# Layer 0's router logits as extra columns of the value and output projections, in a two-layer MetaFormer kernel

## The chip, the cores and the metric

The kernel runs on one core of a Trainium2 chip. A core has five engines that work beside each other, each on its own queue in order: TensorE (PE; its weight loads are shown as PEld), VectorE (DVE), ScalarE (ACT), GpSimd (POOL) and SyncE (SP), which here only issues DMAs. PE writes its results to PSUM, which has eight banks; VectorE and ScalarE evict them from there. The metric is the device time of one execution in microseconds (us), the median over runs. All data is float32 unless said otherwise.

## The reference

The input x has the shape (2, 256, 56, 56): two images, 256 channels, 3136 positions each, so 6272 tokens. Layer 0 computes

```
x = x + attention(ln_c(x))          # 8 heads of 32, window 7 x 7, projections wq wk wv wo with biases
t = tokens(x)                        # (2, 3136, 256)
u = ln_t(t)
logits = u @ router_w.T              # 8 experts
p = softmax(logits); the two largest, normed by their sum
t = t + u + sum over the two experts of p * (gelu(u @ w1 + b1) @ w2 + b2)
```

with `ln(v) = (v - mean) / sqrt(var + eps)` over the 256 channels (eps 1e-6 in ln_c, 1e-5 in ln_t). Layer 1 has two ternary 3 x 3 convolutions with batch norm in the place of attention, and again 8 experts (hidden size 512), of which each token takes two. Only layer 0 is touched by the change.

Two identities matter for it. A layer norm ahead of a linear map can be put behind it: with a matrix whose columns have mean zero, the mean drops out, and the norm is a factor per token. And attention's output enters the logits through wo alone, so `router_w` times `wo` can be multiplied once, ahead.

## The kernel before, in words

The image is cut into 14 strips (`STRIPS`, 7 per image) of 8 rows, that is 448 tokens, held as 4 blocks (`NTT`) of 112 (`TT`) tokens on the partitions.

*Attention (`score_*` and `att_*` pools).* The loop over strips g runs 8 chunks each (4 blocks of 14 columns times 2 halves of the heads). A chunk is `scores` (matmuls sc, two exponentials ex on ScalarE) and `attend` of the chunk before (matmuls av, added into `acc` by VectorE). Beside the chunks two kinds of generators are advanced, one step per chunk, up to their next `yield`: `project(g + 2)`, which norms a coming strip, turns it (px), and computes keys, queries (both pj) and values (pv); and everything in `under_way`, advanced by `push`. There `leave(g - 1)` finishes a strip behind: it loads its x again (`again`: xr plus the bias of wo, on POOL), writes the softmax denominators to DRAM (sums), loads them in another layout (den), inverts them (rden), sends them back out (shares) and loads them spread (rec), multiplies `acc` by them (oc, 8 VectorE operations), resets the strip's rows of `acc` for the second image (`fresh`), multiplies by wo (pw) and adds xr. Then `norm` of `routing(0)` norms the tokens (statistics on VectorE, the root as a power on POOL, scaling to u on ScalarE), turns u by 8 transposes (pu, evicted by two ScalarE copies), stores x + u as x_mid, and computes the logits with 8 matmuls (pl) of 8 columns, whose result VectorE copies to `lgs`. `settle`, for two strips at a time, finds the two best experts of each token on VectorE, counts places with small matmuls (rk), and scatters each token's row into the experts' list xs: 16 indirect DMAs on POOL, two a step (strips 12 and 13 are settled alone, 8 each).

The PSUM tiles with tag aux (px, pj, pv, pw, pu, pl, rk) take turns on two banks. pv and pw fill a bank with two blocks of 256 columns; VectorE evicts the two blocks of pv in two operations, those of pw in one of 512 columns.

*Experts of layer 0.* The rows of strips 0 to 9 (`FIRST`) are enough to know 27 tiles (`EARLY`) of 256 rows that one expert will surely have. They are planned (`plan_first`, `tiles0(0)`) as soon as these strips are counted, and the expert stage starts with them while strips 10 to 13 still go through `leave`, `norm` and `settle`: `beside(j)` advances `under_way` by one step per tile. When nothing is under way any more, `routed_all` plans the remaining 28 tiles (counts, and one small matmul pf behind the whole plan), frees attention's memory, and the preparation of the convolution weights (`ternary`) begins beside the tiles, with loads of the raw weights on SP and sums on ScalarE (low). Per tile, SP loads rows (xg, four tiles ahead) and weights (w, three tiles ahead), PE turns the rows (pt), multiplies twice (ph, py), VectorE adds the bias (y), and POOL scatters y to ys with two indirect DMAs. The order inside this stage is written out by hand; in the attention stage each engine's order is set by a scheduler from the program's order, which is the order of the steps above.

After that come the convolutions (from 835 us) and layer 1's experts, which the change doesn't touch.

Of the kernel before, what the change touches and what calls it, by code (L numbers as in the profile page):

```python
# [10 lines left out]
F32 = mybir.dt.float32  # L11
# [4 lines left out]
ALU = mybir.AluOpType  # L16
# [4 lines left out]
P = 128  # L21
# [608 lines left out]
def metaformer(ctx: ExitStack, tc: tile.TileContext, a: dict, out: bass.AP, flag):  # L630
# [98 lines left out]
    def routing(layer, wp, tp, ps):  # L729

        pre = f"L{layer}_ffn_"
        gate = wp.tile([P, KC, E], F32, tag="gate", name="gate")
        nc.sync.dma_start(gate, a[pre + "gate"].rearrange("(k p) e -> p k e", p=P))
        if layer == 1:
            gate_b = wp.tile([TT, E], F32, tag="gate_b", name="gate_b")
            nc.sync.dma_start(gate_b, a[pre + "gate_b"].partition_broadcast(TT))
# [11 lines left out]
        def norm(i, src, late=False):  # L748


            eng = nc.vector if late else small_eng
# [5 lines left out]
            scaled(u, src, rstd, nmr)  # L757
            yield
# [10 lines left out]
            if layer == 0:  # L769
                eng.tensor_tensor(src, src, u, ALU.add)  # L770
                nc.sync.dma_start(x_mid[i], src)
                yield
            lg = lgs[:, i * NTT : (i + 1) * NTT, :]
            pl = ps.tile([TT, NTT, E], F32, tag="pl" if layer else "aux", name="pl")
# [9 lines left out]
            if layer == 1:  # L784
                yield
                nc.vector.tensor_tensor(lg, pl, bcast(gate_b, 1, [TT, NTT, E]), ALU.add)
            else:
                nc.vector.tensor_copy(lg, pl)
# [209 lines left out]
        return norm, settle, tiles, gates, wgt, counted, sent  # L998
# [294 lines left out]
    with ExitStack() as st:  # L1293
# [22 lines left out]
        def again(g, eng):  # L1316

            xr[g] = tp.tile([TT, NTT, C], F32, tag="xr", name="xr")
            nc.sync.dma_start(xr[g], a["x_tok"][g])
            eng.tensor_tensor(xr[g], xr[g], bcast(bias["o"], 1, [TT, NTT, C]), ALU.add)  # L1320

# [3 lines left out]
        for n in "kqvo":  # L1325
            wt[n] = (aw if n == "o" else sw).tile([P, KC, C], F32, tag=f"w{n}", name=f"w{n}")
            nc.sync.dma_start(wt[n], a[f"L0_conv_w{n}"].rearrange("(k p) o -> p k o", p=P))
# [15 lines left out]
        nc.vector.tensor_copy(far_w.rearrange("p h w -> p (h w)"), far_f)  # L1343
        fits = aw.tile([TT, DEN], F32, tag="fits", name="fits")
# [18 lines left out]
        norm0, settle0, tiles0, gates0, wgt0, counted0, _ = routing(0, aw, tp, ps)  # L1363

        def project(g):
# [39 lines left out]
            for t in range(0, NTT, 2):  # L1405
                pj = ps.tile([TT, 2, C], F32, tag="aux", name="pv")
                for i in range(2):
                    for k in range(KC):
                        nc.tensor.matmul(  # L1409
                            pj[:, i, :],  # L1410
                            xc[:, k, (t + i) * TT : (t + i + 1) * TT],
                            wt["v"][:, k, :],
                            start=k == 0,
                            stop=k == KC - 1,
                        )
                for i in range(2):
                    nc.vector.tensor_tensor(
                        vals[g % 3][:, t + i, :, 0::3, :],
                        pj[:, i, :].rearrange("p (j i d) -> p j i d", i=2, d=HD),
                        bias["v"].rearrange("p (j i d) -> p j i d", i=2, d=HD),  # L1420
                        ALU.add,
                    )
                yield
# [54 lines left out]
        def leave(g):  # L1478
# [11 lines left out]
            rden = tp.tile([TT, DEN], F32, tag="rden", name="rden")  # L1490
            for i in range(2):
# [7 lines left out]
            nc.vector.reciprocal(rden, den)  # L1499
            nc.sync.dma_start(shares.rearrange("i (p n) -> (i p) n", n=DEN), rden)  # L1500
# [6 lines left out]

            fit = tp.tile([TT, DEN], F32, tag="fit", name="fit")
            nc.vector.tensor_scalar(fit, den, LEAST, None, ALU.is_ge)
            nc.vector.scalar_tensor_tensor(fit, den, MOST, fit, ALU.is_le, ALU.mult)  # L1510
            nc.vector.tensor_tensor(fits, fits, fit, ALU.add)
# [3 lines left out]
            for i in range(2):  # L1515
                at = slice(3 * HD * i, 3 * HD * i + HD)
                for j in range(2):
                    to = HD * (2 * j + i)
                    for k in range(KC):
# [5 lines left out]
                        )  # L1525
            if g < NS:
                fresh(s)
            yield
            for t in range(0, NTT, 2):
                pw = ps.tile([TT, 2, C], F32, tag="aux", name="pw")  # L1530
                for i in range(2):
                    for k in range(KC):
                        nc.tensor.matmul(  # L1533
                            pw[:, i, :],
                            oc[:, k, (t + i) * TT : (t + i + 1) * TT],
                            wt["o"][:, k, :],
                            start=k == 0,
                            stop=k == KC - 1,
                        )
                x = xr[g][:, t : t + 2, :]  # L1540
                nc.vector.tensor_tensor(x, pw, x, ALU.add)
# [28 lines left out]

        fresh(0)
# [3 lines left out]
        finish(project(1))  # L1575
        before = None
# [24 lines left out]
        while not plans0:  # L1601
            push()
            plan_first()
# [78 lines left out]
    with mid:  # L1682
# [133 lines left out]
        with ExitStack() as both:  # L1816
# [45 lines left out]
            norm, settle, tiles, gates, wgt1, _, sent = routing(1, wp, tp, ps)  # L1862
# [197 lines left out]
```

## Time and profile before

| what | value |
|---|---|
| runs, median of 6 | 1781.97 us (1775.02 to 1783.38) |
| profiled execution, its own time | 1774.22 us |
| its span, first to last instruction | 1772.4 us |
| mean granted TensorE clock | 0.899 |
| busy PE, PEld, DVE, ACT, POOL | 1529.9, 1208.7, 933.1, 712.4, 672.6 us |
| first px (strip 0) | 17.37 us |
| px of strip 13 | 419.80 us |
| first pt, layer 0's experts | 512.18 us |
| first and last issue of a late row's scatter | 576.45 and 652.49 us |
| first convolution matmul | 835.0 us |

The busy times are of one profiled execution and are averages over stages with different limits, so the stage has to be looked at before a share says anything. In the lists below, a line gives the engine, the line of the kernel, the operation and its tiles as out<-in; "us, times, longest" in a list of waits is the total, the number and the longest; matmuls of float32 appear as two records each (pv, pw, pl, pj), transposes as one.

### The profile page before, as it was taken

What the parts mean: (1) busy time and instruction counts of PE and PEld (TensorE: products, weight loads), DVE (VectorE), ACT (ScalarE), POOL (GpSimd) and SP (SyncE); (2) the same over time, 40 slices, a digit from 0 to 9 for tenths busy, and PEclk for the clock granted to TensorE, in tenths of its full rate; (3) what the DMA queues carried; (4) which work ended last, traced back from release to release, by engine and by line L of the source; (5) the groups of instructions that cost most, each with busy time, mean ns of one, the idle gap of its engine ahead of it and who ended that gap; (6) DMA issues with size and microseconds to landing.
All of it is one profiled execution on the core that took longest, in us unless ns stands there. A gap on an engine that the chain in (4) does not pass through costs nothing.

```text
span 1772.4 us, 26006 instructions
## 1 busy us (share of the span) xinstructions
PE 1529.9 (86%) x8709; PEld 1208.7 (68%) x8709; DVE 933.1 (53%) x2621; ACT 712.4 (40%) x1388; POOL 672.6 (38%) x676
## 2 busy tenths in 40 slices
PE   5999997999988958893899899967669999999964
PEld 3555664555567847782678788857558888888843
DVE  3457665566645437875788555568761111111136
ACT  2444442443433424643655452235434333333312
POOL 2111634335343763451455134316765222222210
PEclk9999997999879988996999999975669999999975
DMA  7122424122157967886552000024557877788758
GB/s 231 46 66 86 126 92 131 56 62 75 57 189 237 304 216 249 310 273 176 166 157 73 0 1 1 1 65 129 172 193 259 281 269 270 268 275 284 265 165 307
DMA packets 91886, 291.77 MB, mean 165 GB/s; under 512 B 20487, under 2 KB 35803, under 8 KB 80416
## 3 DMA queue, kind: packets, MB, share of 16 engines
q1 hardware_dynamic: 66736, 231.79, 41.1%
q0 software_dynamic: 21200, 51.82, 8.2%
q10 hardware_dynamic: 3808, 6.42, 1.0%
q8 instruction: 70, 1.15, 0.3%
q14 instruction: 72, 0.59, 0.1%
HBM read 218.51 MB, written 74.20 MB: 165 GB/s over the span
## 4 chain that ended last, share of the span: by engine, by line
PE 62%; DVE 14%; DMA 10%; issue 7%; POOL 4%; ACT 2%; SPq 1%; POOLq 0%; DVEq 0%; ACTq 0%
PE ph L1091 14%; PE py L1108 13%; PE pc L1753 12%; PE av L1464 4%; PE sc L1435 3%; PE pj L1387 3%; PE pw L1533 3%; DVE oc L1520 3%; PE pv L1409 3%; PE pt L1059 2%; DMA got<-ys 2%; DMA out<-o_out 2%; PE pl L777 2%; POOL ys L1118 1%; DVE t_stats L700 1%
## 5 line engine op out<-in xcount | busy, mean ns | idle before, releaser
L1091 PE MATMUL ph<-ut,w 128*128 128x256 f32 (+1 forms) x1472 | 309.4, 361 | 1.8 <-DMA w<-in_L_experts 1.8
L1108 PE MATMUL py<-w,h 128*128 128x256 f32 x1288 | 298.1, 380 | 0.0
L1116 DVE TENSOR_TENSOR y<-py,w 128x512 f32<-128x512 f32 (+1 forms) x120 | 76.8, 640 | 405.5 <-PE py L1108 405.1
L1091 PEld LDWEIGHTS ph<-ut,w 128*128 128x128 f32 x1472 | 252.0, 195 | 28.8 <-DMA w<-in_L_experts 2.4
L1753 PE MATMUL pc<-hi,wq 128*128 128x448 f32 x672 | 256.0, 382 | 16.9 <-ACT hi L1724 16.9
L860 POOL DMA_INDIRECT xs<-u,pos x224 | 217.4, 970 | 131.4 <-issue 60.7
L1108 PEld LDWEIGHTS py<-w,h 128*128 128x128 f32 x1288 | 243.8, 191 | 32.5
L1753 PE MATMUL pc<-lo,wq 128*128 128x448 f32 x672 | 254.9, 380 | 0.0
L1118 POOL DMA_INDIRECT ys<-y,dest x136 | 135.9, 999 | 232.9 <-DVE dest L1066 173.8
L1098 ACT ACTIVATE h<-ph,w 128x256 f32<-128x256 f32 (+1 forms) x368 | 162.9, 448 | 102.1 <-PE ph L1091 98.0
L1454 ACT ACTIVATE ex<-sc 112x476 f32<-112x476 f32 (+3 forms) x224 | 116.3, 571 | 203.9 <-PE sc L1444 197.5
L1063 ACT COPY ut<-pt 128x512 f32<-128x512 f32 (+1 forms) x120 | 65.2, 544 | 281.1 <-PE pt L1059 279.3
L1723 POOL TENSOR_TENSOR v<-pad 128x928 f32<-128x928 f32 (+1 forms) x56 | 98.3, 1761 | 159.6 <-DVE lo L1725 146.9
L1753 PEld LDWEIGHTS pc<-hi,wq 128*128 128x128 f32 x672 | 129.1, 192 | 32.2 <-ACT hi L1724 18.2
L1753 PEld LDWEIGHTS pc<-lo,wq 128*128 128x128 f32 x672 | 129.3, 192 | 15.4 <-DVE lo L1725 1.0
L1464 PE MATMUL av<-ex,vals 112*64 112x238 f32 (+3 forms) x896 | 124.0, 399 | 12.7 <-DVE acc L1474 12.5
L1118 POOL DMA_INDIRECT ys<-y,to x81 | 84.4, 1041 | 128.0 <-DVE dest L1066 65.8
L1474 DVE TENSOR_TENSOR acc<-av,acc 128x238 f32<-128x238 f32 (+3 forms) x224 | 87.8, 408 | 68.2 <-PE av L1464 66.3
L1464 PEld LDWEIGHTS av<-ex,vals 112*64 112x64 f32 x896 | 56.6, 142 | 61.9 <-issue 25.9
L1724 ACT CAST hi<-v 128x928 fp32r<-128x928 f32 x56 | 54.1, 966 | 110.4 <-PE pc L1753 104.2
L1435 PE MATMUL sc<-q_im,keys 32*112 32x238 f32 (+3 forms) x896 | 91.5, 428 | 2.2 <-ACT ex L1454 2.0
L713 POOL TENSOR_TENSOR t_rstd<-t_mv,eps 112x4 f32<-112x4 f32 x26 | 5.6, 217 | 208.8 <-DVE t_mv L702 208.8
(237 smaller groups left out, 2267.5 us busy)
## 6 DMA issues: line engine op xcount, KB each, us to landing
w<-in_L_experts SPq DMA_DIRECT2D x64, 1154.0 KB
w<-in_L_experts SPq DMA_DIRECT2D x56, 641.0 KB
xg<-xs SPq DMA_DIRECT2D x97, 260.0 KB
got<-ys SPq DMA_DIRECT2D x28, 896.0 KB
acc<-in_fresh SPq DMA_DIRECT2D x14, 896.0 KB
xt<-in_x_tok SPq DMA_DIRECT2D x14, 448.0 KB
xr<-in_x_tok SPq DMA_DIRECT2D x14, 448.0 KB
rec<-shares SPq DMA_DIRECT2D x28, 224.0 KB
```

The costliest lines, as they stand in the source:

```text
L860: w = nc.gpsimd.indirect_dma_start(xs[:, :], bass.IndirectOffsetOnAxis(ap=pos[:, j, t0 + t : t0 + t + 1], axis=0), us[t // NTT][:, t % NTT ...
L1091: nc.tensor.matmul(ph[:, :g], w1[:, k, f * P : (f + 1) * P], d["ut"][:, k, :g], start=k == 0, stop=k == KC - 1,)
L1098: nc.scalar.activation(d["h"][:, f, :g], ph[:, :g], AF.Gelu, bias=b1[:, f : f + 1])
L1108: nc.tensor.matmul(py[:, i, :], d["h"][:, f, i * P : (i + 1) * P], w2[:, f, :], start=f == 0, stop=f == NF - 1,)
L1116: nc.vector.tensor_tensor(y[:, :gp], py[:, :gp], bcast(b2, 1, [P, gp, C]), ALU.add)
L1118: o = nc.gpsimd.indirect_dma_start(ys[:, :], bass.IndirectOffsetOnAxis(ap=d["to"][:, i : i + 1], axis=0), y[:, i, :], None, bounds_check=T ...
L1435: nc.tensor.matmul(sc[h // 2][:, h % 2, :nq], keys[g][p, c, tx * TT : (tx + 1) * TT], q_im[p, c, r0:r1, c0:c1], start=True, stop=False,)
L1454: nc.scalar.activation(e[:, :, :nq], sc[j][:, :, :nq], AF.Exp, scale=HD**-0.5)
L1464: nc.tensor.matmul(av[VW * i : VW * (i + 1), :nq], vals[g % 3][:, tx, 2 * c + j, 2 * i : 2 * i + 2, :].rearrange("p a d -> p (a d)"), ex[j ...
L1474: nc.vector.tensor_tensor(d, av[:, :nq].rearrange("p (h w) -> p h w", w=c1 - c0), d, ALU.add)
L1723: (nc.gpsimd if u else nc.vector).tensor_tensor(v[:, :, at : at + n, :], *r, op)
L1753: nc.tensor.matmul(pc[:, :NT], wq[:, k, c, dx * C + o * P : dx * C + (o + 1) * P], part[:, k, :, dx : dx + W], start=m == 0, stop=m == 2 * ...
```

## The change

1. `norm` of layer 0 no longer turns u and multiplies it by the gate: pu, its two copies, pl and its copy are gone. `lgs` of a strip is instead multiplied by rstd (on POOL, on VectorE for strips 12 and 13), and x_mid is stored in a step of its own.
2. wv and wo get 8 columns more (256 + 8). Those of wv are the gate with its column means taken off (`gates_of_values`), those of wo are wo times these (`gates_of_output`); both are made once, at the start, with 8 small matmuls (pg, po, pb) and a load of wo's rows. pv and pw are then 264 columns wide and fill one bank per block, four banks a strip each instead of two.
3. Each bank has two evictions, both on VectorE: the 256 columns as before, and the 8 columns into `lgs` (for pv times the strip's standard deviation `dev`, for pw added). `again` adds the part of the bias `lg_b` to `lgs`, on POOL.
4. In `leave`, for strips 0 to 9 (`calm`), xr's load has a step to itself, ahead of the step that issues sums and den, and the step that inverts den ends there; shares and rec are issued in the next. `fresh` moves behind the yield that follows oc.
5. The expert stage is begun when strip 9's rows are all scattered in the program's order, not when the first plan exists.

```diff
@@ norm
+            lg = lgs[:, i * NTT : (i + 1) * NTT, :]
+            if layer == 0:
+                eng.tensor_tensor(lg, lg, bcast(rstd, 2, [TT, NTT, E]), ALU.mult)
+                yield
+                eng.tensor_tensor(src, src, u, ALU.add)
+                yield
+                nc.sync.dma_start(x_mid[i], src)
+                return
             yield
             ut = tp.tile([P, KC, NT], F32, tag="ut", name="ut", bufs=1)
...
-            if layer == 0:
-                eng.tensor_tensor(src, src, u, ALU.add)
-                nc.sync.dma_start(x_mid[i], src)
-                yield
...
@@ again
+            lg = lgs0[:, g * NTT : (g + 1) * NTT, :]
+            eng.tensor_tensor(lg, lg, lg_b, ALU.add)
@@ at the start
+        wo_rows = parts[:, 2:].rearrange("p a j n -> p (a j n)")[:, : KC * C]
+        free = wt["v"][:, :, C:]
+        def gates_of_values():
+            pg = ps.tile([P, E], F32, tag="aux", name="pg")
+            for k in range(KC):
+                nc.tensor.matmul(pg, ones, gate[:, k, :], start=k == 0, stop=k == KC - 1)
+            nc.vector.tensor_scalar_mul(mean, pg, -1.0 / C)
+            nc.vector.tensor_tensor(free, gate, bcast(mean, 1, [P, KC, E]), ALU.add)
+        def gates_of_output():
+            nc.sync.dma_start(wo_rows, a["L0_conv_wo_rows"].rearrange("(k p) c -> p k c", p=P))
+            nc.sync.dma_start(bo, a["L0_conv_bo"])
+            po = ps.tile([P, KC, E], F32, tag="aux", name="po")
+            for k in range(KC):
+                for o in range(KC):
+                    nc.tensor.matmul(po[:, k, :], wo_rows[:, o, k * P : (k + 1) * P], free[:, o, :], ...)
+            nc.vector.tensor_copy(wt["o"][:, :, C:], po)
+            for k in range(KC):
+                nc.vector.tensor_scalar_mul(gate[:, k, :], free[:, k, :], bo[:, k : k + 1])
+            pb = ps.tile([TT, E], F32, tag="aux", name="pb")
+            for k in range(KC):
+                nc.tensor.matmul(pb, ones[:, :TT], gate[:, k, :], start=k == 0, stop=k == KC - 1)
+            nc.vector.tensor_copy(lg_b, bcast(pb, 1, [TT, NTT, E]))
@@ project
-            for t in range(0, NTT, 2):
-                pj = ps.tile([TT, 2, C], F32, tag="aux", name="pv")
...
+            nc.vector.reciprocal(dev, rstd)
+            for t in range(NTT):
+                pj = ps.tile([TT, C + E], F32, tag="aux", name="pv")
...
+                nc.vector.tensor_scalar_mul(lgs0[:, g * NTT + t, :], pj[:, C:], dev[:, t : t + 1])
+                if t % 2:
+                    yield
@@ leave
+            calm = g < FIRST[0]
+            if calm:
+                yield
             for i in range(2):
                 nc.sync.dma_start(sums[i : i + 1, :]...
...
             nc.vector.reciprocal(rden, den)
+            fit = tp.tile([TT, DEN], F32, tag="fit", name="fit")
...
+            if calm:
+                yield
             nc.sync.dma_start(shares.rearrange("i (p n) -> (i p) n", n=DEN), rden)
...
+            yield
             if g < NS:
                 fresh(s)
-            yield
-            for t in range(0, NTT, 2):
-                pw = ps.tile([TT, 2, C], F32, tag="aux", name="pw")
...
-                nc.vector.tensor_tensor(x, pw, x, ALU.add)
+            for t in range(NTT):
+                pw = ps.tile([TT, C + E], F32, tag="aux", name="pw")
...
+                nc.vector.tensor_tensor(x, pw[:, :C], x, ALU.add)
+                lg = lgs0[:, g * NTT + t, :]
+                nc.vector.tensor_tensor(lg, pw[:, C:], lg, ALU.add)
@@ after the loop over strips
-        while not plans0:
+        while FIRST[0] - 1 not in sent0:
             push()
             plan_first()
```

## The prediction

> **What bounds the kernel now.** I read the slices of the page first, then the busy time by stretch, then TensorE's instructions in order through one strip, then the waits of layer 0's expert stage. The slices (40 of 44.3 us each; a digit is the busy share in tenths, of the clock the share granted):
>
> ```profile
> PE   5999997999988958893899899967669999999964
> DVE  3457665566645437875788555568761111111136
> ...
> PEclk9999997999879988996999999975669999999975
> ```
>
> In the attention stage (slices 1 to 11) PE is at 9 and VectorE at 4 to 7. By stretch (columns: stretch, length, busy PE, PEld, DVE, ACT, POOL with counts, granted clock, DMA share, GB/s):
>
> ```profile
> 99.65:132.13 32.48, 32.48 (x243) 19.31 (x241) 20.31 (x57) 15.69 (x31) 7.36 (x8) 1.00 0.29 88
> 278.50:327.00 48.50, 37.25 (x202) 23.53 (x199) 32.31 (x73) 14.70 (x29) 14.95 (x17) 0.72 0.31 95
> 419.80:512.18 92.38, 78.69 (x556) 47.78 (x554) 58.59 (x167) 28.83 (x57) 37.91 (x43) 0.83 0.30 94
> 576.45:653.43 76.98, 61.95 (x327) 54.05 (x326) 34.02 (x142) 29.74 (x55) 59.27 (x62) 0.91 0.78 261
> ```
>
> The first row is one strip: PE busy without a gap, DVE 20 of 32 us. A strip lasts as long as its matmuls. The order inside it:
>
> ```profile
> 111.35 3.71 PE L1533 MATMUL pw<-wo,oc 128*112 128x256 f32 x16
> ...
> 116.79 1.98 PE L1409 MATMUL pv<-wv,xc 128*112 128x256 f32 x8
> 118.70 0.67 PE L1435 MATMUL sc<-q_im,keys 32*112 32x238 f32 x8
> ...
> 125.87 0.99 PE L763 MATMUL pu<-ident,u 112*128 112x112 f32 x8
> 126.79 0.76 PE L1435 MATMUL sc<-q_im,keys 32*112 32x280 f32 x8
> ...
> 128.55 1.74 PE L777 MATMUL pl<-gate,ut 128*112 128x8 f32 x16
> 130.22 0.76 PE L1435 MATMUL sc<-q_im,keys 32*112 32x280 f32 x8
> ```
>
> From start to next start, pu holds PE for 0.92 us and pl for 1.67, inside the gapless strip. In the expert stage POOL is the full engine (59.27 us busy of 76.98 in the last row above); its work there:
>
> ```profile
> L860 POOL DMA_INDIRECT xs<-u,pos x32 | 30.8, 961 | 12.5 <-issue 9.7 <-DMA xs<-u,pos 0.6 <-DVE hot L808 0.6
> L1118 POOL DMA_INDIRECT ys<-y,dest x28 | 28.1, 1004 | 8.2 <-issue 5.8 <-DVE t_stats L700 0.3 <-DVE y L1116 0.3
> ```
>
> 60 issues with 0.3 us between them fill the stretch. Behind it PE stands still twice, the second time because ScalarE is held by the conv weights' load:
>
> ```profile
> PE pf L1633 <- DVE unfit_b L1631: 12.4, 1, 12.4
> PE pt L1059 <- ACT ut L1063: 10.1, 3, 7.6
> ```
>
> ```profile
> 663.90 0.63 ACT L1238 ACTIVATE low<-x 128x512 f32<-128x512 f32 x1 [11.01 <-DMA x<-in_L_conv_w_flat]
> ```
>
> **The change, part by part.** The sum is made against the profiled execution, 1774.2 us (span 1772.4 and 1.8 around it). The runs' median is 1782.0, 7.8 above it; I add this difference at the end.
>
> *Logits as columns, to px of strip 13 (419.80).* Nine strips (0 to 8) pass pu and pl before that point: 9 x 2.59 = -23.3. Eight columns more: a pv record of 256 columns takes 1.91/8 = 0.239 us, so 8 columns 7.5 ns; 16 records per projection and strip make 0.12, for 13 pv and 9 pw: +2.6. The weights folded at the start are 16 short records, like one pl: 1.7, and px now follows a matmul on the gate's load. That load is issued at 14.13; its neighbour hot took 3.4 to land, so 17.5 against px's 17.37; +0.8, at most 3: together +2.5. The rows of wo (256 KB) and bo pass ahead of strip 3's xt on SP's queue and are needed only by matmuls some 20 us later; xt arrives strips ahead, so nothing. ScalarE loses two copies a strip (534 ns each), which is worth nothing, since it was 16 of 32 us busy.
>
> *Evictions.* VectorE gets eight instructions of 112x8 a strip and a reciprocal. No row has them: the nearest is lgs<-pl, 112x32, 192 ns; the far ones are 112x4 (about 160) and 112x256 (418). I take 0.19: +1.7. Four evictions of 112x256 (418) for two of 112x512 (689) add 0.3; the lgs copy goes, -0.2. DVE goes from 20.3 to 22.1 of some 30 us, so on average it is hidden under PE. Locally not quite: in the built order pw follows pv at once, six banks in a row of 0.97 us each over two buffers, while DVE does 0.42 + 0.19 + statistics 0.42 + 0.16 per bank: 0.2 us short each, and oc (4.65 us a strip) stands between them. I take 0.45 a strip, 9 x 0.45 = +4; ends 0 (cover holds) and 2.5 a strip = 22 (half of oc in the open). POOL's two new additions of 112x32 are about 0.25 each (xr<-xr,bo, 112x1024, is 2.35): it was 7 to 13 busy per strip; the product with rstd stands ahead of nmr there, so u starts 0.25 later, inside the step that norm has in hand.
>
> Sum to 419.80: -23.3 + 2.6 + 2.5 + 4 = **-14**.
>
> *Transfers a step behind.* sums (2) and den, shares and rec (2) are issued a step later; on SP's queue xr now passes before sums, x_mid after the next sums, rec after xt, fresh one step later. What SP no longer holds back are loads made strips ahead, so I cost this at nothing: x_mid is read first at 822, fresh six strips later. The cover is the spare step; if it is gone, oc waits up to the 3.2 us that DVE's longest wait for rec has now. One step more per strip below 10; one less in norm.
>
> *From px of strip 13 to the first expert tile (92.38 now).* Both pu/pl pairs here go, but scattering the early rows becomes the end of this part, because two more pushes come before the experts. px, two pj, two pv, pw(9) and four chunks: 0.9 + 6.4 + 3.9 + 3.8 + 7.1 + 1.4 (DVE) = 23.5. Eight chunks of 1.78 are 14.2, but strip 10's transfers take from 451.5 (xr issued) to 469.45 (pw), 18: pw(10) at +43.5, ends 47.3, chunk and rk 49.6. Then 2.5 to the first scatter (between 1.1 of DVE work and the 4.5 seen at 473.1 to 477.6), 16 x 1.25 and an addition of 2.36, 2.0 landing, and xg to pt 5.7 (506.44 to 512.18): 82.2. **-10**, between 0 (the wait moves only) and -18 (PE alone).
>
> *The expert stage.* In the built order the first late scatter follows 12 ys instead of 18, and the second plan comes after 21 tiles instead of 23. Before: first late scatter 64.3 after the first pt (576.45), last 141.2. After: first py at 8.3, three tiles of 3.89, pw and rk 4.1, two tiles, 2 to POOL: +34. The same 60 issues take 77: +111. The conv load waits for these scatters; PE went on 11.7 after the last (653.43 to 665.16), with 25 tiles done. After: 122.7 with 23 done, and two tiles, 130.5, against 153.0: -22.5. The 12.4 us for the plan stays inside. I take **-20**; ends -28 (three pu/pl pairs, 6.8, count too) and 0 (POOL starts as late as now).
>
> Sum: -14 - 10 - 20 = **-44**: 1730 for such an execution, **1738** as a median. Nothing after 803 is edited.
>
> [...] Where PE stood still for 7.16 us before pw, at 278.53, the stretch behind it has clock 0.72 (second row above). [...]
>
> **The rivals.**
> B, attention gains, the experts don't: the late rows keep their place since POOL still waits for y and the plan. For it: POOL's first late scatter waited for things that the profile doesn't name. Against: the first late rk follows 4 tiles instead of 7. -24: 1758.
> C, VectorE becomes attention's bound: the stall is 2.5 a strip, +22 instead of +4, and the tail gains only 5, the experts 16: (-23.3 + 2.6 + 2.5 + 22) - 5 - 16 = -17: 1765. For it: the stretch 278.50:327.00 has DVE at 32 of 48 us with PE stalled. Against: 20 of 32 in a plain strip.
> D, the later transfers also remove stalls: the 48.5 us of 278.50:327.00 shrink to the 32.5 of a plain strip. -44 - 16: 1722.
> E, the other side: slower by one mechanism. The first operation of each settle now stands on VectorE right behind the statistics and waits for POOL's product of lgs and rstd, which stands behind 16 scatters. From one strip's rstd to the next POOL needs 1.8 + 20 + 2.4 + 2.4 + 0.6 + 1.8 = 29, against 30 us of a strip: 1 us to spare. With scatters at 2 us instead of 1.25 each of five settles holds DVE 11 us and the av banks with it: 55 - 44 = +11: 1793. It decides from 9 us a settle. For it: thin slack. Against: the scatters kept 1.25 in every burst now.
> That the change does nothing is excluded: pu and pl are gone from the program.
>
> **How the numbers follow.** A 0.55, B 0.15, C 0.13, D 0.07, E 0.10. The time is A's; its own range is 1724 to 1752 (stall 0 to 1.5 a strip, experts -10 to -28). The range 1712 to 1770 takes in B, most of C and D, and leaves out E and the edges. Some 0.2% (3.6 us) is what a measurement can tell. A, B, D and nearly all of C are faster: 0.87; same 0.03 (C's edge); slower 0.10.
>
> **What the profile after would show.** pu and pl gone in layer 0; px to px some 30 us instead of 32.5 in strips with pw; px of strip 13 near 406; first pt near 488; first late scatter near 522 (576.45 now); first conv matmul near 791 (835.0 now). Wrong if DVE's evictions show waits of PE pv or pw over 1 us a strip, if most waits for POOL, or if PE's wait before pt grows.

## The result, and the profile after

The changed kernel takes 1802.56 us (median of 20 runs, 1794.37 to 1810.05), the kernel before 1778.92 (46 runs). The ratio is 1.0127, 95% interval 1.0108 to 1.0146: slower by 1.3%, where 2.5% faster was forecast. Measured once more (r_after below) it was 1.0106 (1.0066 to 1.0145).

The two profiled executions, cut at the same points of the work (us):

| from - to | before | after | difference | forecast |
|---|---|---|---|---|
| start to px of strip 4 | 99.65 | 102.08 | +2.4 | +2.5 |
| px of strip 4 to px of strip 13 | 320.15 | 336.22 | **+16.1** | -16.7 |
| px of strip 13 to the first pt | 92.4 | 96.5 | +4.1 | -10 |
| first pt to the first convolution matmul | 322.8 | 315.5 | -7.3 | -20 |
| from there to the end of the span | 937.4 | 944.1 | +6.7 | 0 |
| span | 1772.4 | 1794.4 | +22.0 | -44 |

(The forecast's -14 to px of strip 13 is +2.5 for the start and -16.7 for the rest, rounded.) The second row holds half of the miss (33 of 66 us). The slices of the page of after (40 of 44.9 us; tenths busy, for PEclk tenths of the full clock granted):

```profile
PE   6998988999778868893889899977779999999953
...
DVE  4456566664765447864787556568761111111146
...
PEclk9999988899879989996899989965569999999975
```

In the attention stage (slices 1 to 11) PE is below 9 in five slices, where it was in two, and the clock in five, where it was in three. The same stretch by busy time, first before, then after (columns as in the prediction: stretch, length, busy PE, PEld, DVE, ACT, POOL with counts, clock, DMA share, GB/s):

```profile
99.65:419.80 320.15, 300.16 (x2198) 180.99 (x2197) 202.16 (x581) 138.82 (x271) 121.01 (x141) 0.95 0.30 91
```

```profile
102.08:438.30 336.22, 299.65 (x1982) 164.83 (x1980) 210.70 (x672) 129.09 (x253) 125.65 (x157) 0.89 0.28 84
```

216 matmul records are gone (72 of pu, 144 of pl). By the prediction's own prices that is -23.3 + 2.6 = -20.7 us, so PE should be busy 279.5; it is busy 299.65. By these prices the remaining matmuls take 20.2 us longer, at a mean clock of 0.89 instead of 0.95. (By the clock column alone, 0.11 of 336 us is lost instead of 0.05 of 320, some 21 us more.) And PE's idle time goes from 20.0 to 36.6 (length less busy). -20.7 + 20.2 + 16.6 = +16.1, the whole row.

What PE waits for there (total us, times, longest), before and after:

```profile
PE av L1464 <- DVE acc L1474: 8.8, 6, 2.2
PE pw L1533 <- DVE oc L1520: 7.2, 1, 7.2
PE pw L1533 <- DVE q_im L1399: 3.5, 5, 1.2
PE sc L1435 <- ACT ex L1454: 0.2, 1, 0.2
```

```profile
PE sc L1486 <- ACT ex L1505: 18.1, 9, 2.4
PE pv L1457 <- DVE q_im L1446: 8.4, 9, 2.2
PE av L1515 <- DVE acc L1525: 6.4, 9, 1.4
PE pv L1457 <- DVE lgs L1470: 2.8, 2, 2.1
```

pw no longer waits for oc. In its place sc waits for ex, 2.1 to 2.4 us in eight of the nine strips. One such place in the timelines of after (start, us, instruction, in brackets the idle time ahead and its releaser), PE, then POOL, then ScalarE:

```profile
158.12 3.80 PE L1589 MATMUL pw<-wo,oc 128*112 128x264 f32 x16
161.85 0.68 PE L1486 MATMUL sc<-q_im,keys 32*112 32x238 f32 x8
...
162.56 1.02 PE L1515 MATMUL av<-ex,vals 112*64 112x238 f32 x8
165.85 0.92 PE L1486 MATMUL sc<-q_im,keys 32*112 32x238 f32 x6 [2.27 <-ACT ex L1505]
```

```profile
163.14 0.20 POOL L713 TENSOR_TENSOR t_rstd<-t_mv,eps 112x4 f32<-112x4 f32 x1 [3.95 <-DVE t_mv L702]
163.42 1.02 POOL L714 TENSOR_TENSOR t_rstd<-t_rstd,minus_half 112x4 f32<-112x4 f32 x1
164.51 0.20 POOL L715 TENSOR_TENSOR t_nmr<-t_nmr,t_rstd 112x4 f32<-112x4 f32 x1
```

```profile
164.75 0.60 ACT L721 ACTIVATE u<-xr,t_nmr,t_rstd 112x256 f32<-112x256 f32 x1 [8.29 <-POOL t_nmr L715]
165.25 1.00 ACT L1505 ACTIVATE ex<-sc 112x476 f32<-112x476 f32 x2
```

The scores were finished at 162.6 (the matmuls left out above), but ex stands behind u in ScalarE's queue, and u waits for the statistics of pw's result: VectorE until 163.3, POOL until 164.7. The next scores need the PSUM banks that ex frees. The step behind for the transfers is what put this in the open. leave has two steps more, so pw, on the queries' step in the kernel before, now falls on the last step of pv, and the four chunks behind it have no other matmuls. Before, pv covered this chain, and pu and pl stood in those chunks.

Behind each such gap the granted clock falls as well (same columns as above; each pair is a gap and the stretch behind it):

```profile
126.69:128.96 2.27, 0.01 (x2) 0.01 (x2) 0.45 (x2) 1.11 (x3) 1.23 (x3) 1.00 0.01 3
129.50:136.30 6.80, 6.80 (x46) 3.29 (x48) 1.63 (x4) 3.40 (x7) 2.35 (x1) 0.50 0.23 70
163.59:165.86 2.27, 0.01 (x2) 0.01 (x2) 0.82 (x4) 1.11 (x3) 1.23 (x3) 1.00 0.00 0
167.10:170.50 3.40, 3.21 (x20) 1.38 (x20) 3.24 (x5) 1.63 (x5) 2.35 (x1) 0.50 0.04 9
```

A gap of 2.27 us is followed, 0.5 or 1.2 us later, by 6.8 or 3.4 us at 0.50. All 12 gaps of 2 us or more between 90 and 470 us of this trace (2.1 to 2.5 us) have a stretch at 0.50, of 3.4 to 17.1 us, that begins no later than 3 us behind them.

The stages behind, to be read against the rows of before: a strip, the stretch from px of strip 13 to the first pt, and the late scatters:

```profile
102.08:137.86 35.78, 33.14 (x219) 17.56 (x217) 21.21 (x66) 14.60 (x29) 5.63 (x9) 0.90 0.23 69
438.30:534.83 96.53, 73.29 (x509) 40.31 (x507) 64.11 (x188) 28.51 (x57) 41.25 (x48) 0.83 0.35 105
579.80:663.10 83.30, 62.32 (x308) 53.10 (x308) 40.20 (x152) 28.60 (x55) 59.22 (x62) 0.89 0.85 288
```

The strip has 219 matmul records instead of 243, and takes 35.78 us instead of 32.48. In the second row PE has 5.4 us less to do than before and the stretch is 4.1 longer. In the third POOL is busy 59.22 us as before, in 83 us instead of 77.

### The profile page after: what moved, and what is told of

It is laid out like the page before. It is cut to its first block, busy times and chain, and to the rows that moved or that the text cites. A ratio compares the mean times of both kernels' runs of the same rounds, so it can differ in the third digit from the quotient of the medians.

```text
span 1794.4 us, 25576 instructions
## 1 busy us (share of the span) xinstructions
PE 1531.1 (85%) x8389; PEld 1187.5 (66%) x8389; DVE 951.5 (53%) x2771; ACT 698.5 (39%) x1360; POOL 679.2 (38%) x700
## 4 chain that ended last, share of the span: by engine, by line
PE 35%; DMA 7%; DVE 6%; issue 2%; ACT 2%; POOL 2%; SPq 0%; ACTq 0%; DVEq 0%; POOLq 0%
PE pc L1813 12%; PE ph L1092 10%; PE py L1109 10%; DMA got<-ys 3%; PE pt L1060 1%; DMA out<-o_out 1%; DMA x_on<-x_mid 1%; DVE x_on L1173 1%; DVE t_stats L700 1%; PE pl L781 1%; DMA xs<-u,pos 1%; POOL xs L861 1%; PE pu L1184 1%; POOL x_on L1177 1%; PE pu L772 0%
## 5 line engine op out<-in xcount | busy, mean ns | idle before, releaser
L1813 PE MATMUL pc<-hi,wq 128*128 128x448 f32 x672 | 256.3, 382 | 16.7 <-ACT hi L1784 16.7
L1119 POOL DMA_INDIRECT ys<-y,dest x136 | 135.1, 993 | 254.0 <-DVE dest L1067 172.0
L1515 PE MATMUL av<-ex,vals 112*64 112x238 f32 (+3 forms) x896 | 135.0, 426 | 18.2 <-DVE acc L1525 17.9
L1813 PEld LDWEIGHTS pc<-hi,wq 128*128 128x128 f32 x672 | 129.1, 193 | 32.1 <-ACT hi L1784 18.1
L1486 PE MATMUL sc<-q_im,keys 32*112 32x238 f32 (+3 forms) x896 | 100.2, 464 | 21.4 <-ACT ex L1505 21.3
L1486 PEld LDWEIGHTS sc<-q_im,keys 32*112 32x112 f32 x896 | 44.9, 192 | 72.9 <-ACT ex L1505 42.8
```

Source lines behind the costliest of these rows:

```text
L1119: o = nc.gpsimd.indirect_dma_start(ys[:, :], bass.IndirectOffsetOnAxis(ap=d["to"][:, i : i + 1], axis=0), y[:, i, :], None, bounds_check=T ...
L1486: nc.tensor.matmul(sc[h // 2][:, h % 2, :nq], keys[g][p, c, tx * TT : (tx + 1) * TT], q_im[p, c, r0:r1, c0:c1], start=True, stop=False,)
L1515: nc.tensor.matmul(av[VW * i : VW * (i + 1), :nq], vals[g % 3][:, tx, 2 * c + j, 2 * i : 2 * i + 2, :].rearrange("p a d -> p (a d)"), ex[j ...
L1813: nc.tensor.matmul(pc[:, :NT], wq[:, k, c, dx * C + o * P : dx * C + (o + 1) * P], part[:, k, :, dx : dx + W], start=m == 0, stop=m == 2 * ...
```

## The experiments

T1: the place of pw and u in the strip, set by the step behind, is the loss. T2: VectorE's double evictions hold the banks. T3: the later start of the experts. The runs went to different chips. On two of them (e1 to e4 on one, e6 to e9 on the other) the kernel before takes 1932.66 and 1922.86 us, and the engines pause for nothing that the profile shows; on the others it takes 1779 to 1781. Ratios are each against the kernel before on the same chip, and times and waits are compared within one kind of chip.

**The step behind undone, or made alone; the start alone.** e1 (and r_calm_off) is

```diff
-            calm = g < FIRST[0]
+            calm = False
```

e2 adds to the kernel before the two `if calm: yield`, the reset behind the yield, and the start:

```diff
+            calm = g < FIRST[0]
+            if calm:
+                yield
...
-        while not plans0:
+        while FIRST[0] - 1 not in sent0:
```

e4 has only these last two lines, and e3 one yield ahead of u:

```diff
             rstd, nmr = yield from token_stats(tp, src, eps5, layer == 1 or late)
+            if layer == 0 and not late:
+                yield
```

> The changed kernel with its transfers where they were (calm is never true): the logits stay columns, both evictions stay on VectorE, the experts' later start stays. Theory T1 (the step behind puts pw on the step of pv; ScalarE's u then waits for POOL's nmr with ex queued behind it, and TensorE has only plain chunks there): the 21.3 us that PE's sc waits for ex fall below 6, the half-rate time before px of strip 13 falls from 72 us to some 30, and px of strip 13 comes near 405 instead of 438; 1765 to 1775 us, ratio to before 0.99 to 1.0. Rival T2 (VectorE's double evictions hold the PSUM banks): the eight small operations a strip are still there, so the time stays at 1795 to 1805. Rival T3 (the loss is the later start of the experts): also 1795 to 1805, with px of strip 13 unchanged from before's 420.

> The kernel before with the step behind alone: xr's load, den and shares a step later for strips 0 to 9, the reset of acc behind the yield, and, because the rows are then written later, the experts' start behind the last row of strip 9. pu and pl stay. Theory T1: slower than before, by 15 to 35 us (1794 to 1814), with 15 us or more of sc waiting for ex, which before had 2.0. Rival T2 (evictions): within 5 us of before, 1775 to 1785. Rival T3 (later start): 10 to 20 slower, but with px of strip 13 still near 420.

> The changed kernel with one more step between nmr and u for layer 0's strips that are not late, so that ScalarE meets u one chunk later; nothing else is moved. Theory T1: sc's waits for ex fall from 21.3 us to under 5, and with them some of the half-rate time; 1780 to 1792. Rival T2: unchanged, 1797 to 1808. A form between: the waits go but VectorE's statistics or settle take their place (acc waits above 25 us instead of 17.9): 1795 to 1805.

> The kernel before with the experts' later start alone (behind the last row of strip 9, not behind the first plan). Theory T1: the tail before the first expert tile grows by 5 to 10 us and the experts give part of it back, so 1779 to 1786. Rival T3: 1790 to 1800, most of the loss that the whole change showed.

Measured: e1 0.9935 (0.9904 to 0.9966), e2 1.0102 (1.0068 to 1.0136), e3 1.0031 (1.0002 to 1.006), e4 0.9989 (0.9951 to 1.0028). The start costs nothing: T3 falls. The step behind slows even the kernel that has pu and pl, by 1.0%, and sc waits 27.5 us for ex in it (100 to 560 us; 9.8 in e1, 14.7 in e4). Not all of this is the same loss as in the change. From px of strip 13 to the first pt, e2 and then e4 show

```profile
471.30:606.70 135.40, 90.80 (x604) 55.00 (x603) 56.91 (x174) 32.52 (x64) 42.75 (x48) 0.77 0.25 75
485.00:586.30 101.30, 75.73 (x557) 45.84 (x555) 54.68 (x164) 30.85 (x60) 27.74 (x31) 0.84 0.24 75
```

In these executions e2 loses its time there, 34 us, 16.2 of them waits of sc for ex. Its stretch from px of strip 4 to px of strip 13 is 371.8 us, shorter than e4's 384.9, of which 28.5 are pauses (8.8 in e2). e3 tests nothing: in the built program u keeps its place in ScalarE's queue, one before the next ex, in most strips, and its waits for ex were 34.2 us.

**The three kernels on one chip.**

> The changed kernel once more, so that its profile stands beside the other three on one chip. Ratio to before 1.008 to 1.017 (its interval was 1.011 to 1.015); PE's sc waits 18 to 28 us for ex between 100 us and the last av.

> The kernel before once more, for its profile on the same chip: ratio 0.997 to 1.003; PE's sc waits under 10 us for ex between 100 us and the last av.

> The changed kernel with its transfers where they were, beside the two above on one chip. Theory T1 (the step behind is the loss, the logits as columns are a gain): ratio 0.985 to 0.998; px of strip 13 at least 10 us ahead of before's of the same chip; PE's sc waits under 10 us for ex. Rival T2 (VectorE's evictions eat the gain of pu and pl): px of strip 13 within 3 us of before's, with acc, lgs or q_im named as what PE waits for by 15 us more than in before.

Ratios 1.0106 (1.0066 to 1.0145), 0.9985 (0.9955 to 1.0015) and 1.0044 (1.002 to 1.0068). T1's numbers fail here: with the step behind undone the columns still gain nothing, and px of strip 13 comes at 446.2, 427.9 and 428.8. T2's form of it fails too, since acc and q_im are not waited for longer than in before. What PE waits for between px of strips 4 and 13 in r_calm_off:

```profile
PE pw L1589 <- DVE oc L1577: 11.4, 3, 7.8
PE av L1515 <- DVE acc L1525: 8.6, 4, 2.4
PE pw L1589 <- DVE q_im L1446: 6.7, 1, 6.7
PE sc L1486 <- ACT ex L1505: 2.8, 1, 2.8
```

The waits for ex are down from 18.2 to 2.8, as T1 says, and pw waits 18.1 us for oc and q_im, 14.4 in r_before. VectorE's oc waits 13.5 us there for rec from DRAM, 7.9 in r_after. (In r_before it is 16.4.) So the step behind does take waits away, and puts others in their place. Without it the shorter strip still runs into the transfers; with it, into ScalarE.

**Both at once, by moving leave.** e5 delays leave of strips 0 to 5 and 7 by three steps, so that pw falls into the empty chunks; e6 (and r_leave6) by six, so that pw is back on the queries' step with slack for the transfers; e7 is e2 with the same six. e10 is e6 with `calm = g < FIRST[0] - 2`.

```diff
-                under_way.append(leave(g - 1))
+                under_way.append(later(3 if g - 1 < 8 else 0, leave(g - 1)))
```

> The changed kernel with leave of strips 0 to 5 and 7 begun three steps later still, so that pw stands in the third of the four chunks that have nothing beside them, and u on the step of the queries' pj (strips 6, 8, 9 and later as they were). Theory T1 (what counts is which step pw and u fall on, not that the transfers come later): ex is waited for less than 8 us, half-rate time falls, and the time is 0.975 to 0.995 of before, below the variant without the step behind. Rival T2: 1.005 to 1.015, since all evictions are still there. Rival T4 (any later leave hurts, because settle and its scatters come later): above the changed kernel, 1.013 to 1.03.

> The changed kernel with leave of strips 0 to 5 and 7 begun six steps later: pw stands where the kernel before has it, between the queries' pj and pv, u two exponentials behind, and the transfers keep their extra steps. Theory T1 (two effects: the place of pw and u in the strip, worth the waits for ex, and the transfers' slack, worth the waits of pw for oc): both are gone, PE's sc waits under 5 us for ex and pw under 5 us for oc between px of strip 4 and px of strip 13, and that stretch takes 292 to 308 us, against 328 of before, 339 of the change, 326 with the transfers undone and 310 with leave three steps later; 0.98 to 0.993 of before. Rival T2 (VectorE's evictions): the stretch stays above 318. Rival T4 (later settle): above 1.0 of before.

> The kernel before (pu and pl stay, no columns) with the same places: the step behind, leave six steps later for strips 0 to 5 and 7, the later start of the experts. It gives the price of the columns alone, at one placement. Theory T1: pu and pl now fill two of the empty chunks where nothing waits; their 23 us in the stretch from px of strip 4 to px of strip 13 are real there, so this is 12 to 25 us slower than the same placement with columns, 0.99 to 1.003 of before. Rival T5 (the columns gain nothing whatever the placement, since TensorE only waits in place of pu and pl): within 5 us of it.

> The placement with leave of strips 0 to 5 and 7 six steps later, once more. Theory T1 (place of pw and u, and the transfers' slack): where TensorE shows no unexplained pauses, 0.980 to 0.995 of before, and below the 0.995 of the placement three steps later. Rival T4 (settle and scatters come too late): 0.998 or more.

> The same with strips 8 and 9 also put back where the kernel before has them (calm only up to strip 7), so that pw and u of no strip stand beside empty chunks. Theory T1: the two strips' waits for ex (2 x 2.2 us and the half rate behind them) go, and the first expert tile comes 4 to 8 us earlier: 3 to 8 us below the kernel run beside it, 0.977 to 0.993. Rival: pw of strips 8 and 9 waits for oc again as it did in strips with the short transfers, and nothing is gained (within 2 us).

The stretch from px of strip 4 to px of strip 13, of the runs on chips without the pauses (PE's waits as totals, us):

| run | ratio (interval) | stretch | PE busy | idle | clock | sc for ex | pw for oc, q_im | av for acc |
|---|---|---|---|---|---|---|---|---|
| r_before | 0.9985 (0.9955-1.0015) | 328.1 | 303.1 | 25.0 | 0.94 | 0.2 | 14.4 | 10.1 |
| r_after | 1.0106 (1.0066-1.0145) | 339.3 | 304.6 | 34.7 | 0.87 | 18.2 | 0 | 5.6 |
| r_calm_off | 1.0044 (1.002-1.0068) | 326.0 | 294.8 | 31.2 | 0.92 | 2.8 | 18.1 | 8.6 |
| e5_leave3 | **0.9949** (0.9923-0.9975) | 310.4 | 285.7 | 24.7 | 0.95 | 10.8 | 1.2 | 2.8 |
| r_leave6 | 1.0046 (1.0018-1.0075) | 323.8 | 290.4 | 33.4 | 0.92 | 2.7 | 1.3 | 17.9 |
| e10_places | 0.9974 (0.9945-1.0003) | 319.9 | 289.8 | 30.2 | 0.92 | 2.9 | 3.4 | 17.7 |

e5 keeps all columns and both evictions and is faster than both kernels (1772.32 us against 1780.88 of before), at the upper edge of what T1 said, with more waits for ex than it said (10.8): T2 falls, and so does T4 (a later leave hurts) for three steps. But r_leave6 misses T1's 0.980 to 0.995 and lies where T4 put it (0.998 or more), so for six steps T4 is not ruled out. ex and oc are hardly waited for, and a third wait has come, for acc: oc, pv's evictions and the additions of acc now meet on VectorE. pw also waits 4.6 us for hot, an operation of settle, and rk, settle's matmul, 4.5 for q_im. Each of the places tried trades one wait for another.

e10 misses its forecast too (0.977 to 0.993), but it is 15 us below r_leave6 on the same chip, where 3 to 8 were expected; in the two profiled executions 10.7 us lie between px of strip 13 and the first pt (92.3 against 103.0). Where the steps of two strips fall is worth 0.7%.

On the other kind of chip e6 gave 0.9998 (0.9966 to 1.003) and e7 1.0139 (1.0068 to 1.0211), above T1's 1.003: at one and the same placement the columns are worth 1.4%, 26 us, and T5 (within 5 us) falls. The stretch is 353.9 against 375.2 us in the profiled executions, 21.3 shorter. That this is so near the forecast's -20.7 is partly luck: 14.1 us of e7's stretch and 3.9 of e6's are pauses.

**Is the removed work really free, and what do the evictions cost?** e8 puts five matmuls without use behind pw of strips 0 to 9; e9 makes each small eviction twice.

```diff
+            if calm:
+                cover = ps.tile([P, C], F32, tag="aux", name="cover")
+                for _ in range(5):
+                    nc.tensor.matmul(cover, ident, wt["o"][:, 0, :C], start=True, stop=True)
```

```diff
+                twin = tp.tile([TT, E], F32, tag="twin", name="twin")
+                nc.vector.tensor_tensor(twin, pw[:, C:], lg, ALU.add)
                 nc.vector.tensor_tensor(lg, pw[:, C:], lg, ALU.add)
```

> The changed kernel with five more matmuls of 128x256 behind pw of strips 0 to 9, whose result nobody reads: 10 strips by about 2.4 us, 24 us more of TensorE's work, about what pu and pl were. Theory T1: they lie in the stretch where sc waits for ex, so the time rises by less than 6 us, or falls (ratio to before 1.002 to 1.014). Rival T6 (TensorE's work is the bound and the loss is elsewhere): all 24 us are paid, 1.020 to 1.030.

> The changed kernel with each of the eight small evictions of a strip made twice (0.16 to 0.22 us each, some 1.5 us more of VectorE a strip, 21 in all). Theory T1: VectorE has room, at most 8 us more than the change (1.008 to 1.018). Rival T2 (VectorE's evictions hold the banks): what the first eight cost comes a second time, 15 us or more above the change (1.02 to 1.03).

e8: 1.0083 (1.0054 to 1.0111), e9: 1.0104 (1.0072 to 1.0135). The change itself had 1.0106 and 1.0127, but on the other kind of chip, and the kernel with the step behind undone differs by 1.1% between the kinds (0.9935 and 1.0044), so these ratios alone settle little. The traces say more. e8's 90 records in the stretch, 0.22 us each from start to start, hold PE some 20 us. From pw to the next px, its nine strips take 172.0 us, against 156.4 in after and 156.3 in r_after, with 3.0 us of pauses: more than half of the added work is paid. In two strips it is not. Here they are in e8, then in after:

```profile
120.66:136.18 15.52, 13.95 (x107) 8.62 (x106) 7.47 (x27) 6.19 (x12) 4.22 (x6) 1.00 0.11 33
457.58:474.28 16.70, 14.69 (x116) 9.30 (x115) 8.92 (x39) 6.18 (x12) 9.04 (x11) 1.00 0.15 45
```

```profile
121.20:137.85 16.65, 14.38 (x97) 7.65 (x96) 7.45 (x27) 5.98 (x12) 4.21 (x6) 0.79 0.12 35
421.34:438.30 16.96, 14.82 (x106) 8.32 (x105) 8.42 (x39) 5.98 (x12) 9.79 (x12) 0.80 0.14 43
```

There the waits of sc for ex are 1.6 us at most instead of 2.1 to 2.3, the clock stays at 1.00, and ten more records cost nothing. In four others av waits 2.3 to 2.5 us for acc and the strips are longer than in after. So T6 misses its number (1.020 to 1.030), but that work of the size of pu and pl was free where it stood is not shown. In e8's built order all four parts of u also stand ahead of the next exponentials, where after has one, so more than the matmuls differs. The doubled evictions stay below T2's 1.02, if the change has on this chip what it has on the others, which was not measured; since in the built order they also spread pw's four banks over two steps, they price the evictions only roughly. Against T2, e5 is the firmer evidence.

**Where the experts' gain went.** e12 advances the late strips faster; e11 is e10 with pf and its operations ahead of the second plan.

```diff
         def beside(j):
             push()
+            if j < 7:
+                push()
```

> The changed kernel with what is under way advanced two steps instead of one beside each of the first seven expert tiles: late rows' scatters come some 4 tiles (15 us) earlier, the second plan after 17 tiles instead of 21. No work is added or removed. If the forecast's reading holds (POOL's scatters set when the plan, the convolution's weights and so the convolution come), the first convolution matmul comes 10 to 18 us earlier after the first expert tile than the 315 to 319 of the change, and the time is 1.001 to 1.006 of before. Rival T8 (the stage is the sum of TensorE's work and of waits that only move): within 4 us of the change, 1.009 to 1.014.

> The kernel with the places of all strips, and the matmul pf with its three operations on VectorE ahead of the second plan instead of behind it. Theory T7 (TensorE's 13.8 us before pf are a stall that nothing hides): the wait before pf goes, some 4 us wait for y and the plan remain, and the time falls by 5 to 12 us. Rival: VectorE is busy with the plan all the same, y comes late and TensorE waits for it instead: within 3 us.

e12: 1.0111 (1.0049 to 1.0174), as the change. The last late scatter came 111.6 us after the first pt instead of 128.3, and the first convolution matmul 324.5 after it instead of 315.5 (319.4 in r_after): the scatters alone don't set it (T8, within 4 us of the change, fits), and pw waited 14.1 us for oc, whose transfers had less time. e11: 1.0001 (0.9976 to 1.0026), where e10 had 0.9974. PE's waits from the first pt to the first pc, e10 first, then e11:

```profile
PE pu L1184 <- ACT xn L721: 21.3, 2, 19.7
PE pf L1693 <- DVE unfit_b L1691: 13.8, 1, 13.8
PE pc L1813 <- ACT hi L1784: 9.1, 1, 9.1
```

```profile
PE pu L1184 <- ACT xn L721: 21.6, 2, 19.9
PE pt L1060 <- ACT ut L1064: 16.7, 3, 7.9
PE pc L1813 <- ACT hi L1784: 8.7, 1, 8.7
```

The 13.8 us before pf are gone, and pt waits 16.7 for ut. Waits in this stage change place.

**VectorE under POOL's additions.** In r_leave6 one multiplication of oc, 0.62 us elsewhere, lasted 2.98 beside POOL's addition of 112x1024:

```profile
226.85 0.72 DVE L1525 TENSOR_TENSOR acc<-av,acc 128x238 f32<-128x238 f32 x2
227.60 2.98 DVE L1577 TENSOR_TENSOR oc<-acc,rec 32x448 f32<-32x448 f32 x1
```

```profile
227.72 2.37 POOL L763 TENSOR_TENSOR xr<-xr,u 112x1024 f32<-112x1024 f32 x1
```

e13 is e5, and e14 is e10, with these additions cut in four:

```diff
-                eng.tensor_tensor(src, src, u, ALU.add)
+                for t in range(NTT):
+                    eng.tensor_tensor(src[:, t, :], src[:, t, :], u[:, t, :], ALU.add)
```

> The placement with leave three steps later, and POOL's two additions of 112x1024 (xr plus the bias, xr plus u) made as four of 112x256. Theory T9 (a long addition on POOL holds VectorE's small operations until it ends): VectorE's operations of over 0.95 us that end with such an addition (13 before 530 us, 27 us of excess) go below 4, PE's waits for acc and q_im fall, 0.985 to 0.994 of before against 0.995 without the cut. Rival T10 (they stand side by side by chance, VectorE waits for something else): unchanged within 0.003, or slower by the added instructions.

> The placement of all strips where the kernel before has pw and u, with the same cut of POOL's additions. Theory T9: av's waits for acc fall from 18 us to under 10 and the time from 0.997 to 0.985 to 0.993 of before. Rival T10: within 0.003 of 0.997.

e13: 0.9946 (0.9921 to 0.9972), e14: 1.0006 (0.9984 to 1.0029). Of VectorE's operations between 60 and 530 us that overlap such an addition and last over 0.95 us there are 8 in e13 instead of 13 in e5, the longest 1.52 instead of 3.41 us. And each of the 13 ends 0.02 to 0.08 or 0.47 to 0.49 us behind the addition that it overlaps. So the two go together: such an operation lasts until the addition's end or 0.5 us past it. But four additions of 0.76 us take 3.0 us where one takes 2.36, and the time does not follow: e13 and e5 are alike, 0.5% faster than the kernel before. In e14 there are 12 such operations, as in e10, and av still waits 21.8 us for acc, so it hardly tests T9. That this costs time is not shown.

## Why the prediction was wrong

*The step that failed first* is "Transfers a step behind. ... I cost this at nothing". I looked at what each transfer is needed for, and there the forecast held: nothing was late. I did not follow pw, which is moved by the same two steps (the prediction's "One step more per strip below 10; one less in norm" counts the strip as a whole; pw stands ahead of norm), nor the chain behind it (statistics, POOL's root, u on ScalarE) into chunks that have nothing to cover it. The built order did show pw right behind pv; I read it for VectorE's evictions alone. Priced by the runs, the step behind is 1.0% in e2 (in the profiled execution the loss lies behind px of strip 13) and 0.6% between r_after and r_calm_off (1.0106 against 1.0044), where the stretch is 339.3 against 326.0 us.

*The larger error* is under it: "A strip lasts as long as its matmuls." Two of the nine strips from px of strip 4 on were gapless before (32.48 and 31.72 us), and in r_before PE already waits 14.4 us for oc and q_im and 10.1 for acc. Transfers (18.1 us of waits in r_calm_off), ScalarE (18.2 in r_after) and VectorE (17.9 in r_leave6) each take over, depending on the placement, as soon as 2.3 us a strip of matmuls are gone. The -23.3 + 2.6 was about right as work (216 records gone; PE busy 299.8 us in e6's stretch, 324.7 in e7's, at clocks of 0.88 and 0.87) and wrong as time. Which engine takes over at each place is read from the waits; how much of the time each of them costs was not separated.

*Evictions.* The stall of +4 was of the right size: pv waits 2.8 us for lgs in the stretch and 8.4 for q_im, av 6.4 for acc, together 17.6, against 8.8 of av and 3.5 of pw before, 12.3. One of the signs of being wrong was there all the same: pv's 11.2 us are 1.2 a strip. C, VectorE as the bound through the evictions, is not what happened in the change; with pw moved back it is near (r_leave6).

*The start*: +2.4 against +2.5, partly by luck: between r_before and r_after it is +7.1.

*px of strip 13 to the first expert tile*: +4.1, past the end of the range (0 to -18). av waits for acc 11.5 us there (17.9 up to the last av, of them 6.4 before px of strip 13), 3.7 before; settle, oc and the additions of acc meet on VectorE there, and the sum had no term for it. PE's wait for xg ahead of the first pt grew from 2.8 to 4.9 us, another of the signs. (Two sums of the prediction are off besides: pw(10)'s parts, 23.5 and 18, give 41.5 and not 43.5, and A's own range, from its own ends, is 1726 to 1758.)

*The experts*: -7.3 instead of -20. The first late scatter came 45.0 us after the first pt (34 forecast, 64.3 before), the last 128.3 (111 forecast, 140.3 before). But the stage gave about what the three pu/pl pairs alone are worth, 6.8 us. I took POOL's full queue for what sets the convolution's start; in e12 the last late scatter comes 16.7 us earlier than in the change, and the convolution no sooner. Rival B's zero is nearer than the forecast.

*E, the slower rival*, had the sign and not the place. most waits for POOL's lgs, 8.4 us in five settles, at most 1.7 each, far from the 9 a settle from which it decides. No rival named ScalarE's queue.

*The clock behind gaps.* The forecast of 1738 us has no term for it; I looked at one gap, of 7.16 us. The gaps behind which the clock fell in the changed kernel are, up to px of strip 13, of 2.1 to 2.4 us. The trace of before had one of this size already, which I did not weigh (the gap, and the stretch at 0.50 that begins within it):

```profile
298.86:301.01 2.15, 0.00 (x0) 0.00 (x1) 2.12 (x4) 1.03 (x2) 0.70 (x1) 0.72 0.32 93
299.82:310.06 10.24, 9.05 (x28) 5.86 (x29) 4.88 (x11) 1.14 (x3) 2.34 (x1) 0.50 0.58 179
```

*Behind the first convolution matmul* +6.7 us, where nothing is edited; r_after against r_before shows +7.2. Some 5 of it lie behind the last scatter of layer 1 (67.8 us to the end before, 72.7 after), where rows are gathered and the output is written. r_calm_off has 71.0 there. From the first convolution matmul to the end, the two profiles of before have 937.4 and 937.7 us, the four of builds without the step behind in strips 8 and 9 (r_calm_off, e10, e11, e14) 939.9 to 942.0, the six with it (after, r_after, e5, r_leave6, e12, e13) 944.1 to 946.2. So it goes with the change, in part with these two strips; its cause was not found, and was not tested.

## What to carry to other kernels

A strip in which one engine has no gap does not show how much slack the others have: before pricing removed matmuls as time, add up the second-longest chain through the strip (here transfers; statistics to u on ScalarE's queue, 18.1 us of waits for ex in the change; VectorE), and forecast no more than the difference. When a step is moved, follow every instruction it issues to its new neighbours, and ask what covers the latency of the chain behind it; small matmuls in otherwise empty chunks can be cover (two strips of e8), and cover is not free everywhere. A placement is itself worth as much as the work: the same columns gave 1.0106, 1.0044, 1.0046 and 0.9949 by where the steps of leave stood.

## What the runs showed of the hardware

- In the changed kernel, gaps of 2.1 to 2.5 us of TensorE between 90 and 470 us went with stretches of 3.4 to 17.1 us at a granted clock of 0.50 (two are shown above). Over the stretch from px of strip 4 to px of strip 13, 16.6 us more idle time came with 20.2 us of longer matmuls. Not every gap of this size did it: later in the same trace, gaps of 2.08 us at 606.70, 2.90 at 868.59 and 2.19 at 912.97 have none within 3 us. And in before a stretch of 3.4 us at 0.50, from 234.97, has no gap of 2 us between the first px and itself (1.54 us at 232.24 is the one before it). What the granted clock follows was not shown.
- A VectorE multiplication ended 0.5 us behind POOL's addition and lasted 2.98 us instead of 0.62 (r_leave6, above); its record begins 0.12 us ahead of POOL's. In the changed kernel's trace 10 operations of VectorE between 60 and 530 us overlap such an addition and last 1.95 to 2.72 us; each ends 0.04 to 0.08 or 0.48 us behind it. One of them is hot, 2.35 us at 167.88 and 0.22 at 165.96. What ties the ends together was not shown.
- On two of the chips the engines paused without a releaser. In e4, PE waited 57.6 us in 30 such places over the span, ScalarE 36.1 and VectorE 28.4; in r_before 0, 10.7 and 9.8. The largest entry of e4's list of waits, over the whole span:

```profile
PE sc L1435 <- issue: 17.4, 6, 7.8
```

- There the kernel before takes 8 to 9% longer, and undoing the step behind gave 0.9935 instead of 1.0044: which placement wins can depend on the chip. What the pauses are stays open, and on PE they are 57.6 of some 150 us.
